# Expert routing by counted places in the first phase, and linear attention with its neighbours as one chain per batch

## Chip, cores, metric

One NeuronCore of a Trainium2 chip runs the whole program in one launch. The metric is the device time of that core in microseconds, the median of several runs; lower is better. The engines, with the names that the profile uses: TensorE (PE for matmuls, PEld for its weight loads), VectorE (DVE), ScalarE (ACT), GpSimd (POOL) and SyncE (SP, which issues most DMAs here; POOL issues the indirect ones). Each engine works off its own list of instructions in order and waits on semaphores for the others.

## What is computed

A stack of eight layers over x of 8 x 512 x 128 (4096 rows of 128 numbers, float32), each as x = x + layernorm(layer(layernorm(x))): softmax attention, a channel mix, a learning recurrence, a switch of experts, linear attention, a mixture of experts in which each expert picks its rows, attention with rotary positions, and a last set of experts. The change touches the three in the middle and the end of the third:

```python
# layer "L1_ffn": each row goes to its best expert, which keeps the first 256 rows that come
logits = x @ w_switch + b_switch
probs = jax.nn.softmax(logits, axis=-1); pmax = probs.max(axis=-1); routes = probs.argmax(axis=-1)
oh = (routes[:, None] == jnp.arange(E)[None, :]).astype(jnp.int32)
pos = (jnp.cumsum(oh, axis=0) * oh).sum(-1) - 1
keep = pos < capacity                                  # capacity = 4096 * 0.5 / 8 = 256
slot = jnp.where(keep, routes * capacity + pos, E * capacity)
buf = jnp.zeros((E * capacity + 1, D), x.dtype).at[slot].set(x)
h = jax.nn.relu(jnp.einsum('ecd,edh->ech', buf_e, w1) + b1[:, None, :])
y = jnp.einsum('ech,ehd->ecd', h, w2) + b2[:, None, :]
out = jnp.where(keep[:, None], y_flat[slot], x) * (pmax / stop_gradient(pmax))[:, None]

# layer "L2_attn": linear attention, 16 heads of 8
q, k = softplus(l2_normalize(q)), softplus(l2_normalize(k))
kv = einsum('bhnd,bhnc->bhdc', k, v) * scale;  ksum = k.sum(2) + EPS
out = einsum('bhnd,bhdc,bhn->bhnc', q, kv, 1 / einsum('bhnd,bhd->bhn', q, ksum))

# layer "L2_ffn": each of 8 experts takes the 512 rows that score highest for it
scores = softmax(xf @ gate_w.T);  vals, idx = top_k(scores.T, 512)
y = layernorm(xf[flat_idx]) * ln_w + ln_b
out = gelu(y @ fc1s.T + b1s) @ fc2s.T + b2s            # scaled by the score, added into xf
```

## The kernel before

Rows lie 128 to a tile; a batch b is 4 tiles (`NJ = 4`), held in SBUF as `cx.x[b]` (128 x 4 x 128) for the whole run. `flip` transposes 4 tiles on PE and copies them out of PSUM on ACT. A layernorm (`stats`, L164) is four bn_stats, four bn_aggr and an add on DVE and then a power on POOL (`ln_rs`, L176); it is applied by DVE (`norm`, L182) or by ACT (`norm_pieces`, L195).

Phase "first" (layers 0 to 3, L1459) has a hand-written order. `Attention.run` puts out the instructions of 128 groups of softmax attention, and between them `Background.pull` lets generators put out a piece each: `residuals`, `Mix.chain`, `Learn.chain` and `Learn.serve_chain`. A batch goes through them one after another; `Learn` is sequential over batches. `serve_chain` is one generator: for each batch in turn it adds the result of the learning layer to x (`served`) and then runs `Route.batch`, so batch b+1 is served behind all that `Route.batch(b)` puts out. `Route.batch` (L859 on) normalizes x, writes it to two tables in DRAM (`l1f_x` and `l1f_out`), and makes the eight logits of each row. When attention has no groups left, `bg.drain()` puts out the remaining pieces of the last batches; that stretch is called the tail here. `load` (L446) loads q, k, v for a group of attention by SP.

Phase "second" has no hand-written order in this version (`ring=0`): a scheduler may reorder within it.

- `l1_ffn` (L961 on): from all logits it finds each row's expert, lists for each expert the numbers of its first 256 rows (`listed`, L896: prefix sums on PE, comparisons on DVE), gathers these rows from `l1f_x` by indirect DMA on POOL (L953), runs the expert, and scatters its rows into `l1f_out` by indirect DMA on POOL (L1018). Then each batch is read back, scaled, normalized and added to x (L1028 to L1032).
- `l2_attn` (L1034 on): stage by stage over all 8 batches: projection for all, square root and reciprocal of all norms at once, exp for all, ln for all with the rest.
- `l2_ffn` (L1097 on): for each batch a layernorm, logits, softmax, a second layernorm scaled by `ln_w`, `ln_b`, and the rows into a DRAM table with their scores; then a search for each expert's 512th score bit by bit (30 rounds, L1152), the list of rows, and the experts with gathers (L953) and adding scatters (L1227).

Of the kernel before, what the change touches and what calls it, by code (L numbers as in the profile page):

```python
# [15 lines left out]
P = 128  # L16
B = 8
# [20 lines left out]
C_ALL = C_ROPE + NJ * 16  # L38
# [20 lines left out]
class Ctx:  # L59
# [104 lines left out]
    def stats(self, src):  # L164

        nc = self.nc
        st = self.common([P, NJ, 6], "ln_st", bufs=6)
        mv = self.common([P, NJ, 2], "ln_mv", bufs=6)
        for j in range(NJ):
            nc.vector.bn_stats(st[:, j, :], src[:, j, :])  # L170
        for j in range(NJ):
            nc.vector.bn_aggr(mv[:, j, :], st[:, j, :])
        ve = self.common([P, NJ], "ln_ve", bufs=6)
        nc.vector.tensor_scalar_add(ve, mv[:, :, 1], EPS)  # L174
        rs = self.common([P, NJ], "ln_rs", bufs=6)
        nc.gpsimd.tensor_tensor(rs, ve, self.mhalf[:, :NJ], ALU.pow)  # L176
        return mv, rs
# [8 lines left out]
    def norm_pieces(self, dst, src):  # L186

        nc = self.nc
        mv, rs = self.stats(src)
        yield 0.0, 1.5  # L190
        yield
        off = self.common([P, NJ], "ln_off", bufs=6)
        nc.vector.scalar_tensor_tensor(off, mv[:, :, 0], -1.0, rs, ALU.mult, ALU.mult)
        for j in range(NJ):
            nc.scalar.activation(  # L195
                dst[:, j, :], src[:, j, :], AF.Identity, bias=off[:, j : j + 1], scale=rs[:, j : j + 1]
            )
        yield
        yield
# [217 lines left out]
def l0(cx: Ctx, at: Attention, Wq, Wk, Wv, mix, learn):  # L417
# [28 lines left out]
    def load(n):  # L446
        b, j = divmod(n, NJ)
        if j == 0:
            bg.drain(projects[b])
            if b == 0:  # L450
                bg.add(mix.load())
                bg.add(learn.load())
            if b + 1 < B:
                projects[b + 1] = project(b + 1)
                bg.add(projects[b + 1])
# [387 lines left out]
class Route:  # L843


    def __init__(self, cx: Ctx, w_switch, b_switch):
        nc = cx.nc
        self.cx = cx
        self.w = cx.const([D, NE], "w1f_sw")
        nc.sync.dma_start(self.w, w_switch)  # L850
        self.bias = cx.row(b_switch, "w1f_bsw")
        self.table = cx.dram.tile([T, D], F32, name="l1f_x", tag="l1f_x")
        self.moved = cx.dram.tile([T, D], F32, name="l1f_out", tag="l1f_out")
        self.logits = cx.const([P, NT, NE], "l1f_logits")
# [4 lines left out]
    def batch(self, b):  # L859
        cx, nc = self.cx, self.cx.nc  # L860
        xn = cx.work([P, NJ, D], "l1f_xn", bufs=1)
        yield from cx.norm_pieces(xn, cx.x[b])
        nc.sync.dma_start(self.by_tile(self.table, b), xn)
        nc.sync.dma_start(self.by_tile(self.moved, b), xn)
# [4 lines left out]
        for j in range(NJ):  # L869
            nc.tensor.matmul(  # L870
                ps[:, j * NE : (j + 1) * NE], xt[:, j * P : (j + 1) * P], self.w, start=True, stop=True
            )
        nc.vector.tensor_add(
            self.logits[:, b * NJ : (b + 1) * NJ, :],
            ps[:, : NJ * NE].rearrange("p (j e) -> p j e", j=NJ),
            self.bias.unsqueeze(1).to_broadcast([P, NJ, NE]),
        )
        yield 0.8


def softmax_parts(cx: Ctx, name, logits):

    nc = cx.nc
    n = logits.shape[1]
    top = cx.work([P, n, 1], name + "_top")
    nc.vector.tensor_reduce(top, logits, AX.X, ALU.max)
    ex = cx.work([P, n, NE], name + "_ex")
    nc.vector.tensor_sub(ex, logits, top.to_broadcast([P, n, NE]))
    nc.scalar.activation(ex, ex, AF.Exp)
    inv = cx.work([P, n, 1], name + "_inv")  # L890
    nc.vector.tensor_reduce(inv, ex, AX.X, ALU.add)
    nc.vector.reciprocal(inv, inv)
    return top, ex, inv
# [67 lines left out]
def l1_ffn(cx: Ctx, route, w1, b1, w2, b2):  # L961
# [3 lines left out]
    cap = T // NE // 2  # L965
    ns = cap // P
    b1c = cx.columns(b1, "w1f_b1")
    b2b = cx.row(b2.rearrange("e d -> (e d)"), "w1f_b2")

    table, moved, logits = route.table, route.moved, route.logits  # L970
    by_tile = route.by_tile

    top, _, pmax = softmax_parts(cx, "l1f", logits)
    scale = cx.work([P, NT, 1], "l1f_scale", bufs=1)
    nc.vector.reciprocal(scale, pmax)
    nc.vector.tensor_mul(scale, scale, pmax)

    eq = cx.work([P, NT, NE], "l1f_eq")
    e8 = cx.c[:, C_E8 : C_E8 + NE].unsqueeze(1).to_broadcast([P, NT, NE])
    nc.vector.tensor_tensor(eq, logits, top.to_broadcast([P, NT, NE]), ALU.is_equal)  # L980
    nc.vector.tensor_mul(eq, eq, e8)
    best = cx.work([P, NT, 1], "l1f_best")
    nc.vector.tensor_reduce(best, eq, AX.X, ALU.min)
    sel = cx.work([P, NE, NT], "l1f_sel", bufs=1)
    nc.vector.tensor_tensor(sel.rearrange("p e t -> p t e"), e8, best.to_broadcast([P, NT, NE]), ALU.is_equal)
    idx = listed(cx, "l1f", sel, cap)
    put = as_indices(cx, "l1f_put", idx)
    nc.vector.tensor_scalar_min(idx, idx, float(T - 1))
    get = as_indices(cx, "l1f_get", idx)

    for e in range(NE):
        we1 = cx.work([D, F], "moe_w1", bufs=3)
        nc.sync.dma_start(we1, w1[e])
        we2 = cx.work([P, NF, D], "moe_w2", bufs=3)
        nc.sync.dma_start(we2, w2[e].rearrange("(f p) d -> p f d", p=P))
        t = cx.tr("l1f_xT_ps")
        for s in range(ns):
            xg = cx.work([P, D], "l1f_xg", bufs=4)
            gather(nc, xg, table, get[:, e, s : s + 1])
            nc.tensor.transpose(t[:, s * P : (s + 1) * P], xg, cx.ident)  # L1000
        xt = cx.work([D, cap], "l1f_xT")
        nc.vector.tensor_copy(xt, t[:, :cap])
        ht = cx.work([P, NF, cap], "l1f_hT")
        for f2 in range(NF // 2):
            hp = cx.big("l1f_h_ps")
            for i in range(2):
                f = 2 * f2 + i
                nc.tensor.matmul(hp[:, i, :cap], we1[:, f * P : (f + 1) * P], xt, start=True, stop=True)
                nc.scalar.activation(ht[:, f, :], hp[:, i, :cap], AF.Relu, bias=b1c[:, f, e : e + 1])
        yp = cx.acc("l1f_y_ps")  # L1010
        for s in range(ns):
            ss = slice(s * P, (s + 1) * P)
            for f in range(NF):
                nc.tensor.matmul(yp[:, ss], ht[:, f, ss], we2[:, f, :], start=(f == 0), stop=(f == NF - 1))
        for s in range(ns):
            y = cx.work([P, D], "l1f_y", bufs=4)
            nc.vector.tensor_add(y, yp[:, s * P : (s + 1) * P], b2b[:, e * D : (e + 1) * D])
            nc.gpsimd.indirect_dma_start(  # L1018
                out=moved,
                out_offset=bass.IndirectOffsetOnAxis(ap=put[:, e, s : s + 1], axis=0),  # L1020
                in_=y,
                in_offset=None,
                bounds_check=T - 1,
                oob_is_err=False,
            )
    for b in range(B):
        o = cx.work([P, NJ, D], "moe_o")
        nc.sync.dma_start(o, by_tile(moved, b))  # L1028
        for j in range(NJ):
            nc.vector.tensor_scalar_mul(o[:, j, :], o[:, j, :], scale[:, b * NJ + j, :])  # L1030
        cx.add_norm(b, o)


def l2_attn(cx: Ctx, W_qkv):  # L1034
    nc = cx.nc
    H = 16
    A = D + H
    w = cx.transposed(W_qkv, "w2a")
    bd = cx.c[:, C_BD : C_BD + A]
    heads = lambda t: t.rearrange("p j (h d) -> p (j h) d", d=8)  # L1040

    qks, vos = [], []
    norms = cx.work([P, B, P], "l2a_n", bufs=1)
    for b in range(B):
        _, xt = cx.normed_flipped(b)
        qk = cx.work([P, NJ, 2 * D], f"l2a_qk{b}", bufs=1)
        vo = cx.work([P, NJ, A], f"l2a_vo{b}", bufs=1)
        nc.gpsimd.memset(vo[:, :, D:], 1.0)
        for j in range(NJ):
            ps = cx.acc("l2a_qkv_ps")  # L1050
            nc.tensor.matmul(ps[:, : 3 * D], xt[:, j * P : (j + 1) * P], w, start=True, stop=True)
            nc.scalar.copy(qk[:, j, :], ps[:, : 2 * D])
            nc.vector.tensor_copy(vo[:, j, :D], ps[:, 2 * D : 3 * D])
        sq = cx.work([P, NJ, 2 * D], "l2a_sq")
        nc.gpsimd.tensor_mul(sq, qk, qk)
        nc.vector.tensor_reduce(norms[:, b, :].unsqueeze(2), heads(sq), AX.X, ALU.add)
        qks.append(qk)
        vos.append(vo)

    nc.vector.tensor_scalar_max(norms, norms, 1e-24)  # L1060
    nc.scalar.activation(norms, norms, AF.Sqrt)
    nc.vector.reciprocal(norms, norms)

    for b in range(B):
        nc.vector.tensor_mul(heads(qks[b]), heads(qks[b]), norms[:, b, :].unsqueeze(2).to_broadcast([P, P, 8]))
        nc.scalar.activation(qks[b], qks[b], AF.Exp)
    for b in range(B):
        sp, vo = qks[b], vos[b]
        nc.scalar.activation(sp, sp, AF.Ln, bias=1.0)
        kv = cx.acc("l2a_kv_ps")  # L1070
        for j in range(NJ):
            nc.tensor.matmul(kv[:, :A], sp[:, j, D:], vo[:, j, :], start=(j == 0), stop=(j == NJ - 1))
# [4 lines left out]
        cx.flip(qt, sp[:, :, :D])  # L1077
        op = cx.big("l2a_o_ps")
        for j in range(NJ):
            at = (j % 2) * A  # L1080
# [450 lines left out]
```

## Time and profile before

| what | us |
| --- | --- |
| median of 3 runs (lowest, highest) | 2361.89 (2356.22, 2367.21) |
| the profiled execution | 2359.79 |
| its span, first to last instruction | 2358.0 |
| start, to the first attention group | 0 to 31 |
| attention with layers 0 to 3 behind it | 31 to 735 |
| tail of the first phase | 735 to 886 |
| lists of rows for `l1_ffn` | 886 to 909 |
| its experts, to the last scatter | 909 to 973.5 |
| its rows added to x | 973.5 to 1018 |
| `l2_attn` | 1018 to 1137 |
| layernorms, logits and table of `l2_ffn` | 1137 to 1211.5 |
| search and list of `l2_ffn` | 1211.5 to 1322 |
| its experts and their sum into x | 1322 to 1505 |
| third phase (layers 6 and 7) | 1505 to 2358 |

The stages are read from the timeline by the first and last instruction that bears a stage's tile names. The clock that the page calls granted is TensorE's alone: 1.00 for most of both attention stretches, 0.5 where PE has little to do.

### The profile page before, as it was taken

To read this page: it belongs to the slowest core of one execution; us is meant where nothing else is said; L and a number is where in the kernel's file an instruction comes from. 1 tells how busy PE (TensorE), PEld (TensorE's weight loads), DVE (VectorE), ACT (ScalarE), POOL (GpSimd) and SP (SyncE) were. 2 spreads that over 40 slices of the span, in tenths; PEclk is the share of its full clock that TensorE was granted. 3 is DMA by queue.
4 is the path that set the end of the run, shared out by engine and by line. 5 is a ranking of instruction groups with operands and counts; after the bars stand their busy time and mean duration, and the time that the engine had idled before them with its cause. 6 is when DMAs were issued, how large, how long until landed. Compare 5 with 4: busy or idle time off the path is not lost. (4 is left out here: it accounts for less than half of the span.)

```text
span 2358.0 us, 31074 instructions
## 1 busy us (share of the span) xinstructions
PE 1880.9 (80%) x11232; PEld 955.4 (41%) x11232; DVE 1351.8 (57%) x4000; ACT 1094.5 (46%) x2178; POOL 479.3 (20%) x703
## 2 busy tenths in 40 slices
PE   6999999999998557144323773399999999999997
PEld 3334434444444446123222541133444444444455
DVE  3567676767765443386766311576565666755522
ACT  2667666565665312024000220056666666656653
POOL 2011121111111113342310264420111110200000
PEclk7999999999999656677555686599999999999999
DMA  3111111110100003100210232200000000000000
GB/s 91 36 32 21 27 31 22 31 36 17 22 19 17 9 30 106 39 9 0 68 33 0 50 50 28 72 1 1 1 1 5 1 5 1 6 1 6 5 6 9
DMA packets 143642, 55.71 MB, mean 24 GB/s; under 512 B 73307, under 2 KB 139527, under 8 KB 143489
## 3 DMA queue, kind: packets, MB, share of 16 engines
q1 hardware_dynamic: 136832, 47.43, 8.0%
q0 software_dynamic: 6656, 6.30, 1.7%
q8 instruction: 89, 1.46, 0.3%
q14 instruction: 65, 0.52, 0.1%
HBM read 31.68 MB, written 22.15 MB: 23 GB/s over the span
## 5 line engine op out<-in xcount | busy, mean ns | idle before, releaser
L336 DVE TENSOR_REDUCE pad_q<-at_s 128x1 f32<-128x512 f32 x1024 | 656.0, 684 | 392.9 <-PE at_st L342 326.0
L345 ACT ACTIVATE at_e<-at_st 128x512 f32<-128x512 f32 x1024 | 557.2, 594 | 402.3 <-PE at_st L342 387.6
L342 PE MATMUL at_st<-at_qm,at_k 32*128 32x512 f32 x2048 | 638.7, 646 | 6.6 <-DVE pad_q L336 5.8
L335 PE MATMUL at_s<-at_k,at_q 32*128 32x512 f32 x2048 | 590.2, 656 | 5.4 <-DVE pad_q L336 3.9
L176 POOL TENSOR_TENSOR ln_rs<-ln_ve,mhalf 128x4 f32<-128x4 f32 x136 | 138.0, 1014 | 821.7 <-DVE ln_ve L174 749.7
L354 PE MATMUL at_o<-at_e,pad_v 128*32 128x512 f32 x2048 | 280.1, 614 | 1.5 <-ACT at_e L345 1.4
L335 PEld LDWEIGHTS at_s<-at_k,at_q 32*128 32x128 f32 x2048 | 163.0, 188 | 250.8 <-issue 98.9
L342 PEld LDWEIGHTS at_st<-at_qm,at_k 32*128 32x128 f32 x2048 | 185.0, 184 | 60.6 <-DVE pad_q L336 40.8
L1423 PEld LDWEIGHTS l3f_y_ps<-w3f,l3f_hT 128*128 128x128 f32 x1024 | 126.4, 192 | 40.3 <-issue 23.7
L1423 PE MATMUL l3f_y_ps<-w3f,l3f_hT 128*128 128x128 f32 x1024 | 134.7, 278 | 0.8 <-ACT l3f_hT L1417 0.8
L1416 PE MATMUL l3f_h_ps<-l3f_xT,w3f 128*128 128x512 f32 x256 | 131.9, 607 | 1.5 <-ACT l3f_hT L1417 1.5
L354 PEld LDWEIGHTS at_o<-at_e,pad_v 128*32 128x32 f32 x2048 | 41.3, 108 | 199.0 <-issue 153.6
L1417 ACT ACTIVATE l3f_hT<-l3f_h_ps,w3f_b1c 128x512 f32<-128x512 f32 x128 | 87.8, 688 | 65.3 <-PE l3f_h_ps L1416 64.8
L1426 DVE SCALAR_TENSOR_TENSOR l3f_o<-l3f_y_ps,l3f_w,l3f_o 128x128 f32<-128x128 f32 x128 | 44.6, 349 | 118.4 <-PE l3f_y_ps L1423 117.5
L216 PE MATMUL flip<-consts_sb,xn 128*128 128x128 f32 x96 | 23.7, 366 | 100.2 <-DVE xn L182 91.1
L141 PE MATMUL wtr<-consts_sb,raw 128*128 128x128 f32 (+1 forms) x11 | 3.1, 412 | 99.4 <-DMA w3a_b<-in_L_attn_bqkv 67.9
L217 ACT COPY xnT<-flip 128x512 f32<-128x512 f32 x24 | 14.1, 587 | 130.7 <-PE flip L216 105.3
L1225 DVE TENSOR_TENSOR l2f_y<-l2f_y_ps,w2f_b 128x128 f32<-128x128 f32 x32 | 9.1, 290 | 94.0 <-DMA l2f_out<-l2f_y,l2f_get 78.3
L1147 PE MATMUL l2f_count_ps<-l2f_mine,ones 128*128 128x8 f32 x62 | 18.3, 368 | 56.1 <-DVE l2f_mine L1145 56.1
L1227 POOL DMA_INDIRECT l2f_out<-l2f_y,l2f_get x32 | 50.7, 1584 | 53.5 <-DMA l2f_out<-l2f_y,l2f_get 28.6
L216 PEld LDWEIGHTS flip<-consts_sb,xn 128*128 128x128 f32 x96 | 14.9, 166 | 114.2 <-DVE xn L182 58.4
L170 DVE BATCH_NORM_STATS2 ln_st<-x 128x6 f32<-128x128 f32 x256 | 58.1, 277 | 3.2 <-POOL x L838 3.2
(378 smaller groups left out, 2757.0 us busy)
## 6 DMA issues: line engine op xcount, KB each, us to landing
l_qkv<-l_qkv SPq DMA_DIRECT2D x32, 192.0 KB
l_in<-l_qkv SPq DMA_DIRECT2D x96, 64.0 KB
moe_w<-in_L_ffn_w SPq DMA_DIRECT2D x16, 256.0 KB
l2f_x<-l2f_rows SPq DMA_DIRECT2D x8, 272.0 KB
x<-in_L_attn_x SPq DMA_DIRECT2D x8, 256.0 KB
l_o<-l_out SPq DMA_DIRECT2D x32, 64.0 KB
l_y<-l_o SPq DMA_DIRECT2D x32, 64.0 KB
l1f_x<-l1f_xn SPq DMA_DIRECT2D x8, 256.0 KB
```

The source lines that it names most:

```text
L170: nc.vector.bn_stats(st[:, j, :], src[:, j, :])
L176: nc.gpsimd.tensor_tensor(rs, ve, self.mhalf[:, :NJ], ALU.pow)
L335: nc.tensor.matmul(s, qt[n][r, c * P : (c + 1) * P], kt[n][r, :], start=True, stop=True)
L336: nc.vector.tensor_reduce(qp[:, c, h, 8:9], s, AX.X, ALU.max, negate=True)
L342: nc.tensor.matmul(s, kt[n][r, c * P : (c + 1) * P], qm[n][r, :], start=True, stop=True)
L345: nc.scalar.activation(es[g][:, h, :], s, AF.Exp, scale=scale)
L354: nc.tensor.matmul(os[n][32 * h : 32 * h + 32, :], vp[:, c, h, :], e[:, h, :], start=(c == 0), stop=(c == NJ - 1),)
L1227: nc.gpsimd.indirect_dma_start(out=summed, out_offset=bass.IndirectOffsetOnAxis(ap=idx[:, e, s : s + 1], axis=0), in_=y, in_offset=None, c ...
L1416: nc.tensor.matmul(hp, self.w1[:, e, f * P : (f + 1) * P], xt, start=True, stop=True)
L1417: nc.scalar.activation(hts[e][:, f], hp, AF.Relu, bias=self.b1c[:, f, e : e + 1])
L1423: nc.tensor.matmul(yp[:, :D], hts[e][:, f, js], self.w2[:, e, f, :], start=(f == 0), stop=(f == NF - 1))
L1426: nc.vector.scalar_tensor_tensor(o[:, j, :], yp[:, :D], wt[:, j, e : e + 1], o[:, j, :], ALU.mult, ALU.add)
```

## The change

In the first phase `Route.batch` goes on after the logits: softmax parts, the best expert of each row, its place among the expert's rows by matmuls with a triangle and with ones (11 per batch, with a count carried from batch to batch), and four indirect DMAs on POOL that scatter the batch's rows into a DRAM block per expert (`taken`); a row without a place gets a number out of bounds, which is skipped. `clear` writes zeros to `taken` by 8 DMAs of 128 KB on SP, ahead of the first loads for attention. The second copy of the table is gone.

`l1_experts` replaces `l1_ffn`: it loads each expert's 256 rows as a plain block, runs the experts in a hand-written order two steps apart, and stores a plain block (`given`). The lists, the gathers and the scatters of `l1_ffn` are gone. Loads of rows are put out ahead of the loads of weights on SP.

`Pairs.batch` takes together the sum of `l1_ffn` into x, `l2_attn`, and the first part of `l2_ffn`, as one generator of 29 steps per batch. `in_turn` starts a batch every 7 rounds and lets each running batch put out one step per round, the oldest first; this order is kept. Layernorms are applied by ACT throughout; the norms are found by ln and exp instead of square root and reciprocal, with one set of activation functions loaded ahead; squares move from POOL to ACT; `ln_w` and `ln_b` move into the experts' weights in `l2_ffn`.

```diff
 class Route:
...
+    def clear(self):
+        for e in range(NE):
+            self.cx.nc.sync.dma_start(self.taken[e * CAP1 : (e + 1) * CAP1, :]..., self.zero...)
     def batch(self, b):
...
-        nc.sync.dma_start(self.by_tile(self.moved, b), xn)
...
+        top = tile_of("top", 1)
+        nc.vector.tensor_reduce(top, logits, AX.X, ALU.max)
+        ex = tile_of("ex")
+        nc.vector.tensor_sub(ex, logits, top.to_broadcast(by_expert))
+        nc.scalar.activation(ex, ex, AF.Exp)
+        yield 0.8, 0.6
+        eq = tile_of("eq")
+        nc.vector.tensor_tensor(eq, logits, top.to_broadcast(by_expert), ALU.is_equal)
+        nc.vector.tensor_mul(eq, eq, e8)
+        nc.vector.tensor_reduce(best, eq, AX.X, ALU.min)
+        nc.vector.tensor_tensor(sel, e8, best.to_broadcast(by_expert), ALU.is_equal)
+        yield 0.0, 0.6
+        nc.tensor.matmul(ps[:, : NJ * NE], cx.triu, sel.rearrange("p j e -> p (j e)"), start=True, stop=False)
+        for j in range(NJ):
+            for i in range(j + 1, NJ + 1):
+                nc.tensor.matmul(ps[:, i * NE : (i + 1) * NE], cx.ones, sel[:, j, :], start=False, stop=(j == NJ - 1))
...
+        nc.vector.tensor_scalar_add(self.place[:, tiles].unsqueeze(2), best, float(FAR))
+        yield 1.3, 0.9
...
+        for j in range(NJ):
+            nc.gpsimd.indirect_dma_start(out=self.taken, ... in_=xn[:, j, :], ...)
+            yield 0.0, 0.2
...
     def load(n):
         if j == 0:
             bg.drain(projects[b])
             if b == 0:
+                learn.route.clear()
                 bg.add(mix.load())
...
+def l1_experts(cx: Ctx, route, w1, b1, w2, b2):
+    for e in range(NE):
+        xg = cx.work([P, ns, D], "l1f_xg", bufs=NE)
+        nc.sync.dma_start(xg, of_expert(route.taken, e))
...
+    for e in range(4):
+        weights(e)
+    for e in range(NE + 2):
+        if e < NE:
+            taken(e)
+        if 0 <= e - 1 < NE:
+            hidden(e - 1)
+        if 0 <= e - 2 < NE:
+            given(e - 2)
+            if e + 2 < NE:
+                weights(e + 2)
+def in_turn(gens, gap):
+    waiting, running = list(gens), []
+    n = 0
+    while waiting or running:
+        if waiting and n % gap == 0:
+            running.append(waiting.pop(0))
+        for g in list(running):
+            try:
+                next(g)
+            except StopIteration:
+                running.remove(g)
+        n += 1
+class Pairs:
+    def batch(self, b):
+        o = tile_of("o")                                            # steps 1, 2
+        nc.sync.dma_start(o, route.by_tile(route.table, b))
+        for j in range(NJ):                                         # steps 3, 4 (and 5, empty)
+            nc.gpsimd.indirect_dma_start(out=o[:, j, :], in_=route.given, ...)
+        mv = cx.moments(o)                                          # 6: and three small DVE ops
+        rs = cx.root(ve)
+        cx.affine(t, o, rs, cx.offset(mv, rs))                      # 7
+        nc.gpsimd.tensor_add(x, x, t)                               # 8
+        mv, rs = cx.stats(x)                                        # 9
+        cx.affine(xn, x, rs, cx.offset(mv, rs))                     # 10
+        cx.flip(xt, xn)                                             # 11
+        nc.tensor.matmul(ps[:, : 3 * D], xt[:, block(j)], self.w)   # 12, 13: two blocks each
+        nc.scalar.copy(qkv[:, j, : 3 * D], ps[:, : 3 * D])
+        nc.scalar.activation(sq, qk, AF.Square)                     # 14: and four sums, a max on DVE
+        nc.scalar.activation(nf, nf, AF.Ln)                         # 15
+        nc.scalar.activation(nf, nf, AF.Exp, scale=-0.5)
+        nc.vector.tensor_mul(v, v, n[:, j, :]...)                   # 16: four
+        nc.scalar.activation(qk, qk, AF.Exp)                        # 17
+        nc.scalar.activation(qk, qk, AF.Ln, bias=1.0)               # 18
...
+        cx.flip(qt, qkv[:, :, :D])                                  # 19: behind kv and m; 20 is empty
+        nc.tensor.matmul(op[:, k * A : (k + 1) * A], qt[:, block(j)], m)   # 21: and rec, product on DVE
+        mv, rs = cx.stats(o)                                        # 22
+        cx.affine(t, o, rs, cx.offset(mv, rs))                      # 23
+        nc.gpsimd.tensor_add(x, x, t)                               # 24
+        mv, rs = cx.stats(x)                                        # 25
+        rs2 = cx.root(ve)                                           # 26: behind three small DVE ops
+        cx.affine(xn, x, rs, cx.offset(mv, rs))
+        cx.flip(xt, xn)                                             # 27: and the store of xn
+        cx.affine(rows, x, rs2, cx.offset(mv, rs2), D)
+        nc.tensor.matmul(ps[:, j * NE : (j + 1) * NE], xt[:, block(j)], self.gw)   # 28: top, sub, exp
+        nc.sync.dma_start(route.by_tile(self.table, b), rows)       # 29: behind the scores
...
 def l2_ffn(...):
...
         cx.flip(we1, raw1)
+        bp = cx.acc("l2f_b_ps")
+        for f in range(NF):
+            nc.tensor.matmul(bp[:, f : f + 1], we1[:, f * P : (f + 1) * P], lb, start=True, stop=True)
+        nc.vector.tensor_add(be1, bp[:, :NF], b1c[:, :, e])
+        nc.gpsimd.tensor_scalar_mul(we1, we1, lw)
...
     with cx.phase("second"):
+        with cx.layer("layer3", ring=8):
+            l1_experts(cx, route, *of("L1_ffn", "w1", "b1", "w2", "b2"))
+        with cx.layer("layer4", ring=8):
+            tc.keep_in_program_order(nc.scalar.preload_act_table_set("natural_log_exp_and_others"))
+            pairs = Pairs(cx, route, *of("L2_attn", "W_qkv"), *of("L2_ffn", "gate_w"))
+            in_turn([pairs.batch(b) for b in range(B)], 7)
```

The steps of `Pairs.batch` are numbered here for the text; a step is what lies between two `yield`s.

## The prediction

> **What bounds the kernel now.** I read the page's slices first, then busy time by stage, then the timeline where the change works. The slices say whether one engine bounds the whole run:
>
> ```profile
> PE   6999999999998557144323773399999999999997
> DVE  3567676767765443386766311576565666755522
> ACT  2667666565665312024000220056666666656653
> PEclk7999999999999656677555686599999999999999
> ```
>
> PE is full in slices 2 to 12 and in the last 14: those stretches are bound by it. Between them (about 735 to 1505 us) no engine is full and TensorE's granted clock falls to a half: latency and waits set the time. The change works there and adds to the first stretch. By stage (columns: stretch, its length, then busy us and instructions of PE, PEld, DVE, ACT, POOL, then clock, DMA share, GB/s):
>
> ```profile
> 31.00:735.00 704.00, 688.33 (x4360) 300.16 (x4360) 486.92 (x1230) 444.30 (x907) 105.48 (x200) 0.96 0.13 27
> 735.00:886.00 151.00, 89.14 (x429) 68.72 (x427) 61.38 (x245) 43.25 (x99) 25.06 (x25) 0.62 0.08 23
> 886.00:909.20 23.20, 13.77 (x45) 10.14 (x45) 15.78 (x62) 2.96 (x17) 0.76 (x9) 0.50 0.26 77
> 909.20:973.50 64.30, 38.28 (x211) 31.24 (x211) 8.05 (x25) 14.12 (x32) 31.57 (x32) 0.79 0.25 72
> 973.50:1211.50 238.00, 83.48 (x357) 62.19 (x357) 173.40 (x752) 48.40 (x85) 81.47 (x72) 0.63 0.11 33
> ```
>
> The fourth row is bound by none of its engines. The timeline of POOL shows by what:
>
> ```profile
> 965.24 0.98 POOL L1018 DMA_INDIRECT l1f_out<-l1f_y,l1f_put  x1 [2.00 <-issue]
> 968.23 0.98 POOL L1018 DMA_INDIRECT l1f_out<-l1f_y,l1f_put  x1 [2.01 <-DMA l1f_out<-l1f_y,l1f_put]
> 971.14 0.98 POOL L1018 DMA_INDIRECT l1f_out<-l1f_y,l1f_put  x1 [1.93 <-DMA l1f_out<-l1f_y,l1f_put]
> ```
>
> Each scatter waits until the one before it has landed: 3.0 us from start to start though POOL works 0.98. Their data was ready (the last y was written at 961.6). 16 of them make 48 of the stage's 64 us.
>
> **The sum** is made against the profiled execution, 2359.8 us (span 2358.0 and 1.8 around it); the median of the runs, 2361.9, is 2.1 above.
>
> **1. Zeros at the start.** `clear` puts 8 DMAs on SP between the stores of q, k, v (last issue 25.2) and the first loads for attention:
>
> ```profile
> 25.68 4.92 SPq L460 DMA_DIRECT2D l_in<-l_qkv  x9
> 28.12 0.29 POOL L319 COPY pad_q<-l_in 128x128 f32<-128x128 f32 x1 [11.94 <-DMA l_in<-l_qkv]
> ```
>
> A store of 256 KB by SP took 0.36 to 0.51 us to issue (L863, L864), so the loads are issued 8 x 0.43 = 3.4 us later, with 1 MB of zeros before them: in the first 12.5 us about 2.6 MB (constants, x) landed within 10 us, so 1 MB takes about 4 us, mostly under the issues. POOL's copies wait for the loads and the first scores for them; after that PE is full, so nothing makes it up. +5 (3 to 8).
>
> **2. Place-finding inside attention.** `l1f_xn` is stored at 401, 506, 604, 699 and, in the tail, 759, 813, 863, 883: four batches fall under attention. Each adds 11 small matmuls. Nearest are the logits' four (8 records):
>
> ```profile
> 703.47 1.06 PE L870 MATMUL l1f_log_ps<-w1f_sw,l1f_xnT 128*128 128x8 f32 x8
> 884.23 1.88 PE L870 MATMUL l1f_log_ps<-w1f_sw,l1f_xnT 128*128 128x8 f32 x8 [0.68 <-ACT l1f_xnT L217]
> ```
>
> 0.265 us each at full clock, 0.47 at half. 4 x 11 x 0.265 = 11.7 on an engine busy 688 of 704. Some fills gaps: +10 (0 to 12). The 17 DVE operations of some 0.2 us (3.4 per batch) hide under PE while DVE is busy 487 of 704; with PE not full they would cost those 14 us. POOL's scatters stand between `fill` copies put out eight groups ahead and hide too.
>
> **3. Place-finding in the tail.** Here nothing hides: three more batches (4, 5, 6) put 11 x 0.47 = 5.2 us of matmuls into PE's queue, and DVE's next addition waits for them with the learning chain's operations queued behind it. For batches 4 and 5 I take +4 and +5. Batch 6 is worse: batch 7 is served behind it, and its layernorm's power stands in POOL's queue behind batch 6's four scatters:
>
> ```profile
> 874.27 1.01 POOL L176 TENSOR_TENSOR ln_rs<-ln_ve,mhalf 128x4 f32<-128x4 f32 x1 [13.71 <-DVE ln_ve L174]
> ```
>
> Logits of batch 6 at 866.2, choice of experts six small operations to 867.5, matmuls behind each other to 874, places 876, scatters at 876.3, 879.3, 882.3, 885.3: the power comes at 886.4 for 874.3, +12. Sum +20; 8 if the three matmul groups fit PE's idle time, 28 if every wait counts in full.
>
> **4. From the last logits to the experts' last row.** Before: 886.15 to 973.5, 87.3 us. After: choice 1.4, matmuls 5.2, places 1.3, then four scatters at 3.0 and 1.4 to be seen (971.14 + 0.98 to SP's 973.49): 19.7 to the first load of rows. SP then issues 8 loads, b1, b2, and only behind them weights (before, these came at 886.9, ahead of need): 1.8 MB at 260 GB/s from 906 brings the first weights at 915, 9 us on. The experts run at PE's pace of before's unhindered ones, 4.15 us (929.99, 934.14, 938.29 start hidden layers), the first 2.2 more at half clock: 36; addition, store, landing 3. Together 68: -19 (-27 to -12; weights and clock decide). [...]
>
> **5. The chain.** By rows, one batch costs ACT 16.0 us (five affines at 1.65, three copies 0.58, four 0.48, three of 1024 at 1.04, small ones 0.9) where it had 48.4/8 = 6.0; DVE 14.7; POOL 13 (gathers 1.25, powers 1.01, additions 1.27). With four batches in turn the period per batch T is at least 16. The order is kept, so I laid seven rounds out by hand, from the oldest batch's step 23: affine to 1.85; POOL's addition 24 stands behind the power of a younger batch's step 9, which follows the products 16 and its own bn_stats on DVE (3.3): 5.7; stats 25 to 7.2; its power stands behind two gathers (2.5): 9.2; small operations and affine 26: 11.7; ACT's copies 19 and 12: 13.3; copy 27: 13.9; ACT's affine of the rows, two copies, exp, square of step 14: 17.8; four sums of 256 at 0.41 and a max: 19.8; steps 7, 29 and 22 on DVE: 22.3; power: 23.4. At half clock PE's 4 x 1.28 for the projection, 2.2 for kv and so on add 4.5: 27.9. PE would be busy 37%, where 1070 to 1137 (39%) had clock 0.68; T = 25.
>
> The first batch reaches step 23 at 51 (alone but for two young ones), five full periods make 125, the next two, with fewer beside them, 23.5 and 18.5, the last seven steps 14: 232 (219 to 255) for 238 now. -6 (-19 to +17).
>
> **6. Experts of `l2_ffn`.** Each gets one POOL product of 128x512 (between a memset's 0.52 and an addition's 1.27) among scatters 3.6 to 4.1 apart, where gathers already fill most waits; its four matmuls and DVE addition hide under that chain. +3 (0 to +10).
>
> Sum: 5 + 10 + 20 - 19 - 6 + 3 = +13; 2373, beside the median 2374. ±0.5% (12 us) is what a measurement here can tell from no change. The main case's own range is 2358 to 2412.
>
> **Rivals.** *The chain runs at ACT's pace* (T about 17; for it: ACT and DVE alone would allow it, and 29 steps times four batches leave choice; against: the order is fixed and POOL's gathers stand in it): 51 + 7 x 17 + 14 = 184 for 232, 2326. It ends on the faster side as soon as T is under 25 - 25/6.7 = 21.3. *The additions to the first phase vanish* (PE's matmuls fill gaps, the tail takes +6): 10 + 14 less, 2350; for it: PE idles 62 of 151 us in the tail; against: the in-order waits above. *Functions are switched* (exp and ln alternate; the one set does not hold): four loads per batch at the 1.28 of L1066 and L1069, 41 us, of which ACT's slack hides some 5: 2410; against: a set was asked for by name. [...] At L1066 the trace shows the next activation 0.02 us behind the load.
>
> **Chances.** Main case 0.45, T at ACT's pace 0.20, first phase unharmed 0.27, switched functions 0.08. Slower by over 0.5%: 0.36 of the main case, 0.08 of the last, 0.01: 0.45. Faster: 0.18 and 0.11: 0.29. The rest, 0.26, is within. The range takes in most of the faster rival and the bounds above that can meet: 2322 to 2414.
>
> **What will show it.** First scores at 36 instead of 31. Attention's end at 750 and the last logits near 921. Four scatters 3.0 apart behind them, the first transposes of rows about 20 us later. In the chain, powers of step 25 behind gathers on POOL, ACT at two thirds, steps 23 of neighbouring batches 25 us apart (under 21 and I am wrong on the sign), one function load. The search about 13 us later than 1211.5, and the rest unchanged from there but for the experts of `l2_ffn`.

## The result, and the profile after

Twenty runs of each kernel on one chip gave a median of 2374.52 us (2365.75 to 2383.55) for the changed kernel and 2362.14 us (2352.2 to 2367.87) for the one before. The ratio is 1.0056, with a 95% interval of 1.0041 to 1.0072: the change costs some 12 us. The forecast was 2374. The profiled execution of the changed kernel has a span of 2370.5 us (2358.0 before), 12.5 more.

The total hides larger moves. From the first and last starts of a few groups in the two profiles (us):

| stretch | before | after | difference | forecast |
|---|---|---|---|---|
| start to the first scores | 31.1 | 36.2 | +5.1 | +5 |
| attention, to its last output | 718.0 | 736.6 | +18.6 | +10 |
| tail, to the last logits | 137.0 | 152.6 | +15.6 | +20 |
| logits to the first experts' last row | 87.4 | 65.6 | -21.8 | -19 |
| add and linear attention, to the first count of the search | 239.0 | 224.6 | -14.4 | -6 |
| search | 72.1 | 72.1 | 0 | 0 |
| lists, to the first gather | 37.1 | 39.6 | +2.5 | +3 for both |
| experts of `l2_ffn` | 146.7 | 151.6 | +4.9 | |
| sum, start of the third phase | 104.2 | 108.2 | +4.0 | 0 |
| third phase, from its first outputs | 785.4 | 783.4 | -2.0 | 0 |

The page of the changed kernel, its slices (40 equal ones; PE's busy tenths, and the granted clock of TensorE in tenths):

```profile
PE   5999999999999563544333773299999999999998
PEclk7999999999997665766655686589999999999999
```

Attention still fills PE. But the last slice of attention that is full (711 to 770 us) has a clock of 0.7 where it was 0.9. The same kernel by stage (stretch, its length, then busy us of PE, PEld, DVE, ACT, POOL, then clock, DMA share, GB/s):

```profile
36.20:772.80 736.60, 720.35 (x4501) 316.57 (x4502) 498.84 (x1295) 451.72 (x922) 121.14 (x217) 0.94 0.12 25
772.80:925.40 152.60, 88.82 (x443) 75.13 (x441) 67.78 (x292) 37.56 (x90) 37.24 (x36) 0.61 0.03 9
925.40:991.00 65.60, 39.19 (x238) 35.92 (x238) 17.71 (x52) 9.10 (x18) 4.39 (x9) 0.73 0.45 128
991.00:1211.50 220.50, 89.29 (x352) 65.08 (x352) 114.41 (x551) 120.01 (x264) 93.52 (x88) 0.62 0.10 29
```

In the chain (last row) ACT, the busiest engine, works 54% of the time: as before, no engine is full there.

**Attention.** Weighting each 5 us of attention with its granted clock gives the time lost to a clock under 1.0: 26.8 us before, 44.0 after, 17.2 more. PE's work at full clock, what is left of its busy time, is 674.0 and 676.4, its idle time 17.2 and 16.3. By this measure +18.6 is 17.2 of clock and 2.4 of work, less 0.9 of idle time. The kernel before, over the same stretch (to be held against the first row above):

```profile
31.10:749.10 718.00, 700.80 (x4438) 306.14 (x4438) 492.11 (x1248) 452.63 (x923) 107.71 (x203) 0.96 0.12 26
```

The split is a rough one: of PE's 4501 records 88 are new, in four groups that alone hold PE for 11.3 us, while 25 others no longer fall within it. The timeline shows the largest loss, at the fourth group:

```profile
733.14 0.65 PE L332 MATMUL at_qm_ps<-consts_sb,pad_q 128*128 128x128 f32 x4
733.63 0.31 PE L939 MATMUL l1f_rank_ps<-l1f_sel,consts_sb 128*128 128x32 f32 x2
733.78 3.07 PE L944 MATMUL l1f_rank_ps<-l1f_sel,ones 128*128 128x8 f32 x20
736.78 2.08 PE L364 MATMUL at_st<-at_qm,at_k 32*128 32x512 f32 x4
```

and busy time and clock in the stretches of that group and behind it:

```profile
733.60:736.80 3.20, 3.20 (x26) 3.18 (x24) 0.00 (x0) 1.21 (x3) 0.00 (x0) 0.76 0.02 5
736.80:745.00 8.20, 8.20 (x28) 3.53 (x28) 1.10 (x7) 3.33 (x8) 2.03 (x2) 0.50 0.02 7
745.00:757.50 12.50, 12.50 (x42) 4.26 (x46) 5.98 (x22) 4.83 (x10) 2.26 (x2) 0.50 0.06 13
```

Place-finding puts 22 records on PE (11 matmuls, two records each in this trace), 20 of them 8 columns wide. Over the group the clock is 0.76, and behind it 0.50 for 21 us of attention's own matmuls, though PE is busy without a gap: the four `at_st` take 2.08 us instead of 1.13.

**Tail.** Batch 7 behind batch 6's scatters (DVE and POOL):

```profile
903.64 1.04 POOL L968 DMA_INDIRECT l1f_taken<-l1f_xn,l1f_place  x1 [14.82 <-DVE l1f_place L960]
908.10 0.17 DVE L174 TENSOR_SCALAR ln_ve<-ln_mv 128x4 f32<-128x4 f32 x1
912.45 0.97 POOL L968 DMA_INDIRECT l1f_taken<-l1f_xn,l1f_place  x1 [1.96 <-DMA l1f_taken<-l1f_xn,l1f_place]
913.43 1.06 POOL L180 TENSOR_TENSOR ln_rs<-ln_ve,mhalf 128x4 f32<-128x4 f32 x1
```

The variance is there at 908.27; the power that reads it starts at 913.43, in POOL's queue behind the fourth scatter: 5.2 us.

**First experts.** From the last logits (925.4):

```profile
945.02 3.94 SPq L1053 DMA_DIRECT2D l1f_xg<-l1f_taken  x8
949.01 0.41 SPq L161 DMA_DIRECT2D raw_b<-in_L_ffn_b  x1
949.87 0.42 SPq L1065 DMA_DIRECT2D l1f_w<-in_L_ffn_w  x1
951.82 0.57 PE L165 MATMUL col<-consts_sb,raw_b 8*128 8x8 f32 x4 [20.07 <-DMA raw_b<-in_L_ffn_b]
952.32 1.11 PE L1071 MATMUL l1f_xT_ps<-consts_sb,l1f_xg 128*128 128x128 f32 x4
955.70 3.75 PE L1082 MATMUL l1f_h_ps<-l1f_xT,l1f_w 128*128 128x256 f32 x8 [2.27 <-DMA l1f_w<-in_L_ffn_w]
```

The first load of rows is issued 19.6 us behind the logits, the first weights are there at 955.7; then one expert takes 3.73 us (from 963.84 to 967.57).

**Chain.** One period, from one addition L1196 to the next (POOL and DVE alone, in extracts):

```profile
1086.94 1.26 POOL L1196 TENSOR_TENSOR x<-x,l_t 128x512 f32<-128x512 f32 x1
1088.15 1.42 DVE L1233 TENSOR_TENSOR l2a_qkv<-l2a_qkv,l2a_n 128x256 f32<-128x256 f32 x4
1090.91 1.02 POOL L180 TENSOR_TENSOR ln_rs<-ln_ve,mhalf 128x4 f32<-128x4 f32 x1 [2.71 <-DVE ln_ve L174]
1091.90 1.26 POOL L1273 TENSOR_TENSOR x<-x,l_t 128x512 f32<-128x512 f32 x1
1091.96 1.22 DVE L197 SCALAR_TENSOR_TENSOR ln_off<-ln_mv,ln_rs 128x4 f32<-128x4 f32 x1 [1.13 <-POOL ln_rs L180]
1094.70 1.00 POOL L1172 DMA_INDIRECT l_o<-l1f_given,l1f_place  x1 [0.30 <-issue]
1095.72 1.05 POOL L180 TENSOR_TENSOR ln_rs<-ln_ve,mhalf 128x4 f32<-128x4 f32 x1
1102.61 1.00 POOL L180 TENSOR_TENSOR ln_rs<-ln_ve,mhalf 128x4 f32<-128x4 f32 x1 [2.21 <-DVE ln_ve L1189]
1103.67 0.19 DVE L1299 TENSOR_REDUCE l2f_top<-l2f_log_ps 128x4 f32<-128x32 f32 x1 [1.20 <-PE l2f_log_ps L1296]
1110.75 1.26 POOL L1196 TENSOR_TENSOR x<-x,l_t 128x512 f32<-128x512 f32 x1
```

The work passes between DVE and POOL for most of the period; PE and ACT take part too, as at 1103.67, where DVE waits 1.20 us for PE. The power at 1095.72 stands behind two gathers; the small `ln_off` at 1091.96, elsewhere 0.16 us, lasts until POOL's addition ends. The period is 23.8 us.

### The profile page after: what moved, and what is told of

The parts are those of the page before. It is cut to its first block, busy times and chain, and to the rows that moved or that the text cites. A ratio compares the mean times of both kernels' runs of the same rounds, so it can differ in the third digit from the quotient of the medians.

```text
span 2370.5 us, 31595 instructions
## 1 busy us (share of the span) xinstructions
PE 1913.9 (81%) x11432; PEld 987.0 (42%) x11432; DVE 1307.8 (55%) x3890; ACT 1160.3 (49%) x2333; POOL 505.3 (21%) x724
## 5 line engine op out<-in xcount | busy, mean ns | idle before, releaser
L364 PE MATMUL at_st<-at_qm,at_k 32*128 32x512 f32 x2048 | 649.2, 656 | 10.1 <-DVE pad_q L358 9.9
L238 PE MATMUL flip<-consts_sb,l_xn 128*128 128x128 f32 x96 | 26.6, 367 | 121.4 <-ACT l_xn L203 120.3
L238 PEld LDWEIGHTS flip<-consts_sb,l_xn 128*128 128x128 f32 x96 | 14.0, 158 | 139.2 <-ACT l_xn L203 131.9
L203 ACT ACTIVATE l_xn<-x,ln_off,ln_rs 128x128 f32<-128x128 f32 x96 | 39.5, 483 | 48.1 <-DVE ln_off L197 43.8
L334 ACT COPY at_q<-at_q_ps 128x512 f32<-128x512 f32 x64 | 37.7, 589 | 40.8 <-PE at_q_ps L332 40.8
```

The lines of the kernel that those rows point to most:

```text
L238: self.nc.tensor.transpose(t[:, j * P : (j + 1) * P], src[:, j, :], self.ident)
L364: nc.tensor.matmul(s, kt[n][r, c * P : (c + 1) * P], qm[n][r, :], start=True, stop=True)
```

## The experiments

**Places with fewer, wider matmuls.** The ten matmuls of 8 columns per batch become one of 32 for the totals, added up on DVE:

```
-        for j in range(NJ):
-            for i in range(j + 1, NJ + 1):
-                nc.tensor.matmul(ps[:, i * NE : (i + 1) * NE], cx.ones, sel[:, j, :], ...)
+        nc.tensor.matmul(ps[:, NJ * NE : 2 * NJ * NE], cx.ones, sel.rearrange("p j e -> p (j e)"), ...)
+        for j in range(NJ):
+            nc.vector.tensor_add(rank[:, j + 1, :], rank[:, j, :], tot[:, j, :])
```

> The ten matmuls of 8 columns per batch become one of 32 columns, and five small operations of DVE add the totals up (20 fewer instruction records of PE per batch, 1 us more on DVE). Theory A (the short matmuls cost their own time, 2.4 us per batch, and TensorE's clock, which the trace of the changed kernel shows at a half behind all four groups that lie in attention): attention's last output from 772.8 to about 755; each batch of the tail some 3 us earlier; places of the last batch at 4 us behind its logits instead of 7; 2374 falls to 2335 to 2350. Rival B (they cost their own time alone, and the halved clock comes from elsewhere): attention's last output at 764, halved clock behind the places as before; 2350 to 2362. Rival C (attention's length is set by the extra work on DVE and POOL, not by PE): no earlier than 770, and no gain over 8 us.

2356.68 us, ratio to the kernel before 0.9959 (0.9939 to 0.998). Attention's last output at 763.5, the last logits at 906.0 (925.4 in the changed kernel), the last places 4.4 us behind them (7.4). The clock lost in attention is 29.4 us. The size is B's (763.5 for its 764); the mechanism has to be told from the next run, since work and clock both went.

**As many matmuls, but wide.** The same, and nine matmuls per batch of 128 columns whose result nobody reads:

```
+        for i in range(9):
+            nc.tensor.matmul(ps[:, 2 * P : 3 * P], cx.ones, cx.ident, start=True, stop=True)
```

> As the run before, but with nine more matmuls of 128 columns per batch behind the two, whose result nobody reads: as many instructions of PE as in the changed kernel and about the same time of PE (0.117 us a record against 0.107), but 16 times the columns. Theory A (few columns per matmul are what lets the clock fall): the clock stays at full behind the groups in attention, attention's last output at 762 to 767, between the run before and the changed kernel. Rival B (a group of 22 records of any kind, or the stop of attention's own matmuls for 2.4 us, does it): the halved clock stays, last output at 771 to 776.

2374.37 us, ratio 1.0032 (1.0013 to 1.0051). Attention's last output at 764.8, clock lost 31.9. The same group there, and the stretch behind it:

```profile
732.26 2.25 PE L947 MATMUL l1f_rank_ps<-consts_sb,ones 128*128 128x128 f32 x18
734.44 1.13 PE L364 MATMUL at_st<-at_qm,at_k 32*128 32x512 f32 x4
```

```profile
734.50:745.00 10.50, 10.50 (x65) 4.18 (x64) 6.90 (x24) 7.43 (x17) 4.30 (x4) 1.00 0.03 9
```

PE is held for 2.6 us by 22 records as in the changed kernel, and the clock stays at 1.0. Over the profiles: in the changed kernel and the seven others here that keep its groups of 8 columns, a clock of 0.75 or less follows in the 3 us behind 27 of 32 groups in attention; behind the four wide ones it is 1.0 for 12 us, and behind the four short ones of the run before 0.91 or more (two of these fall later: one 3 us on, where the kernel before had a fall too, at 635 to 645, and the last one 6 us on). So in these runs the fall follows groups of 8 columns (27 of 32) and not groups of 128 (none of 4) that hold PE as long: theory A.

It is not the whole of what attention lost. Up to the 30th of its 32 outputs (at 712 us in the kernel before) the three forms lie close together: 12.8 us behind the kernel before with the narrow matmuls, 11.9 with the short, 9.6 with the wide ones, some 5 of it from the start. The last two outputs, with the fourth group among them, add 10.9, 2.5 and 6.1. So that one group in its narrow form costs 5 us more than in the wide and 8 more than in the short one; another 5 to 8 us came with every form, and no run here shows from what. (In the tail, where the changed kernel's clock is 0.50 in each group and in the 3.5 us ahead of it, this profile has 161.7 us, between the 152.5 and 164.4 of the narrow form, and the median can't be told from the changed kernel's.)

**Zeros later.** `clear` is called in front of the second batch's loads.

```
+            if b == 1:
+                learn.route.clear()
```

> The eight stores of zeros move from in front of the first loads for attention to in front of the second batch's. My step 1 (they delay the first loads): first scores at 31 instead of 36.2, and the end 5 us earlier, 2369. Rival (the gain is taken back: in the new place they delay loads that attention waits for, or the first groups' clock swallows it): first scores at 31, but attention's last output at 771 or later.

First scores at 31.4, but attention's last output at 774.0 and the clock lost 47.1 us; 2373.28 us, ratio 1.0043 (1.0021 to 1.0065), which can be told neither from the changed kernel's 1.0056 nor from 5 us (0.2%) less. By its own mark the rival holds, in one profile: the 5 us are real where they arise, and in this execution they were lost by attention's end. By which of its two reasons, and whether the median keeps them, stays open.

**Weights in front of rows.** In `l1_experts` the biases and the first four experts' weights are asked for ahead of the rows.

> In the first experts' stage the first four experts' weights and the biases are asked for ahead of the eight loads of rows on SP's queue instead of behind them. Theory (the first hidden layer at 955.7 waits for weights, my step 4): first hidden layer some 6 us sooner after the last scatter (942.5 to 955.7 is 13.2 us in the changed kernel, 7 here), end at 2368. Rival 1 (the weights' buffers come free only with the last scatter, so that the loads of rows now stand behind weights): 13 us or more, end at 2374 to 2378. Rival 2 (1 MB more in flight beside the row loads delays these by as much as it gains): 11 to 13.

2371.82 us, ratio 1.0034 (1.0013 to 1.0056). Last scatter to first hidden layer 15.5 us instead of 13.2. SP's queue of that run:

```profile
954.20 0.35 SPq L161 DMA_DIRECT2D raw_b<-in_L_ffn_b  x1
955.01 0.42 SPq L1060 DMA_DIRECT2D l1f_w<-in_L_ffn_w  x1
960.14 5.72 SPq L1108 DMA_DIRECT2D l1f_xg<-l1f_taken  x8
```

The last scatter was issued at 951.6. Nothing of the stage is asked for before it has landed, and the rows now come last. The times are rival 1's. But the wait stands at the first load in the queue, the biases', issued 2.6 us behind the last scatter (954.2 for 951.6) as the first load of rows is in the changed kernel (945.02 for 942.46); whether the weights' buffers would have held their loads too, this run doesn't show. (The tail was 164.4 us in this profile, with the very instructions that took 152.6 in the changed kernel's; two more profiles with that code had 152.5, one 164.4. Differences of that size in one profile's tail are no reading.)

**Early weights.** The first four experts' weights get tiles that stay, and are asked for behind the store of batch 6's rows.

> Only the early weights: tiles that stay for the first four experts' weights, asked for behind the store of batch 6's rows, some 60 us ahead of need. Theory (the run with weights ahead of rows lost because the buffers came free only with the first phase's end, not because of the order): places to first hidden layer 16 to 18 us instead of 22.9 in the changed kernel, median 2368. Rival (the loads of rows, the biases' columns and the half clock make the wait, weights or not): 21 or more, median 2374.

2370.74 us, ratio 1.0038 (1.0019 to 1.0057); places to first hidden layer 20.8 us: nearly the rival's. The weights' wait is gone, but PE's first instruction there is the transposes of the biases, whose load stands behind the eight loads of rows (at 949.51; they run at 952.72). The last run moves that load.

**The chain's additions on DVE.**

```
-        nc.gpsimd.tensor_add(x, x, t)
+        nc.vector.tensor_add(x, x, t)
```

> In the chain the two additions of a block to x go from POOL (1.26 us each) to DVE. Theory L (the chain's period, 23.8 us from one batch's addition 24 to the next, is one path that changes between DVE and POOL, in the order the program was written): both additions lie on that path, and DVE's small operation beside each is drawn out from 0.16 to 1.22 us; on DVE an addition of this size takes some 0.7, so the period falls by 1 to 3 us, to 21 to 23, and the chain (first gather to last scores, 220.6 us) to 200 to 213. Rival A (ACT's affines set the period): 23.8 stays. Rival D (DVE is the scarcer engine: 1.4 us more on it per batch): 24 to 25.5, chain 222 to 232.

2353.28 us, ratio 0.996 (0.9938 to 0.9981). The chain takes 210.1 us from first gather to last scores, the period is 22.3 (mean of five). In it:

```profile
1098.85 0.69 DVE L1273 TENSOR_TENSOR x<-x,l_t 128x512 f32<-128x512 f32 x1
1100.43 0.16 DVE L197 SCALAR_TENSOR_TENSOR ln_off<-ln_mv,ln_rs 128x4 f32<-128x4 f32 x1 [0.90 <-POOL ln_rs L180]
```

The addition takes 0.69 and `ln_off` is 0.16 again, in all 40 cases. ACT's work did not change (120.5 us busy for 120.0), so ACT's pace did not set the period. DVE was busy 110.6 us for 114.5: the shorter small operations more than pay for the additions. That is theory L, at its low end. The median gained more than the chain's 10.5 us: by the two ratios to the kernel before some 23 us lie between this run and the changed kernel, and the profile, of the slowest of its ten executions, doesn't show where the rest arose.

**The chain's powers on ACT.**

```
-        self.nc.gpsimd.tensor_tensor(rs, ve, self.mhalf[:, :NJ], ALU.pow)
+        self.nc.scalar.activation(rs, ve, AF.Ln)
+        self.nc.scalar.activation(rs, rs, AF.Exp, scale=-0.5)
```

> In the chain the six powers per batch go from POOL (1.02 us each) to ACT as two activations of 0.3 (a logarithm and an exponential, in the set already loaded). Theory L (DVE and POOL in turn set the period): the path loses up to 0.4 us and the waits behind POOL's gathers and additions at each power, but ACT's affines stand ahead now: 20 to 24. Rival A (ACT sets the period): ACT gets 3.6 us more per batch, period 26 to 28, chain 235 to 250.

2363.39 us, ratio 1.0 (0.9982 to 1.0019). Chain 217.1 us, period 23.4 (mean of five). ACT was busy 132 us instead of 120 and the period did not grow: against rival A again. It hardly fell either; whether what is won behind POOL's gathers is lost behind ACT's affines wasn't separated. Here too `ln_off` takes 0.16 us in 39 of 40 cases (in the changed kernel 12 of 40 take 1.2), so the drawn-out operation alone is not what set the period. By the ratios this run is some 13 us faster than the changed kernel, of which the chain accounts for 3.5; the rest isn't explained.

**Scale on DVE.** In the experts of `l2_ffn` the product `we1 * lw` moves to DVE.

> In the last experts' stage the product of the first weights with the norm's scale (POOL, 1.6 us, eight times) goes to DVE. My step 6 (it stands among POOL's gathers and scatter-adds): first gather 1.6 to 2.8 us sooner after the search's end (39.1 us in the changed kernel, 36.6 before), and the stretch from the first gather to the loads of the sums 147 to 149 instead of 151.6 (146.7 before). Rival (the stretch is longer because of the four added matmuls and the clock): 151 or more.

One run, 2362.65 us. First gather to the loads of the sums 148.0 us: POOL's share is borne out, by a little (nine profiles without this edit have 149.5 to 152.1, the two later runs that have it 146.8 and 147.8). But the first gather came 39.4 us behind the search's last count (39.6 in the changed kernel), no sooner:

```profile
1319.72 0.16 DVE L1397 TENSOR_TENSOR l2f_b<-l2f_b_ps,w2f_b 128x4 f32<-128x4 f32 x1 [1.33 <-PE l2f_b_ps L1395]
1319.91 0.48 DVE L1398 TENSOR_SCALAR l2f_w<-l2f_w,w2f_lnw 128x512 f32<-128x512 f32 x1
1320.31 0.18 DVE L1031 CAST l2f_get<-l2f_idx 128x32 int32<-128x32 f32 x1
```

The first expert's bias addition, which waits for PE, stands in DVE's queue ahead of the conversion that the gathers need; the product has only joined it there.

**Scatters that needn't wait.** Each of a batch's four tiles goes to a table of its own; the experts read the first alone.

> The four tiles of each batch are scattered to four tables instead of one; the experts read only the first of them, so three quarters of the rows that they should get are zeros (the work is the same). Theory W (each scatter waits for the one before it, since all write one table: 2.9 us apart, of which POOL works 0.98): 1.2 to 1.5 us apart, the last batch's four in 4 to 5 us instead of 8.7, and its power no longer 5.2 us late behind the batch before: last scatter 8 to 10 us earlier. Rival Q (POOL's queue or the writing of the descriptors takes 2.9 whatever the target): 2.5 us or more apart, nothing gained.

One run, 2363.74 us. The last batch's scatters:

```profile
932.10 1.03 POOL L971 DMA_INDIRECT l1f_taken<-l1f_xn,l1f_place  x1 [13.41 <-DVE l1f_scale L969]
933.44 0.98 POOL L971 DMA_INDIRECT l1f_part<-l1f_xn,l1f_place  x1 [0.30 <-issue]
934.73 0.97 POOL L971 DMA_INDIRECT l1f_part<-l1f_xn,l1f_place  x1 [0.30 <-issue]
936.00 0.97 POOL L971 DMA_INDIRECT l1f_part<-l1f_xn,l1f_place  x1 [0.30 <-issue]
```

1.3 us apart instead of 2.9: the wait is for the one table (theory W). Places to first hidden layer 18.8 us instead of 22.9. Batch 7's power now follows its variance by 0.09 us instead of 5.2, and from batch 6's logits to batch 7's it is 26.0 us instead of 30.9. The last scatter came 6.5 us earlier, not 8 to 10; the tail as a whole was 155.1 us. This form does not give the right rows, and one that does was not tried.

**The kernel before again.**

> The kernel before once more, to see how far a single profile of it goes. Theory (its first phase is shorter than the changed kernel's because the clock is lost less): attention's last output at 747 to 755, lost clock in attention near 27 us, and no half clock for over 12 us on end after 600. Rival (the first profile was a lucky one): 758 or more.

Attention's last output at 750.4, clock lost 27.4, the tail 137.1: the first profile was no lucky one. From the loads of the last experts' sums to the third phase's first outputs it takes 108.2 us, where the first profile had 104.2. Five profiles with the changed kernel's first phase have 731.6 to 738.1 us in attention (37.8 to 44.9 of them lost to the clock) and 152.5 to 164.4 in the tail.

**Together.** Wider place-finding, additions and scale on DVE, early weights.

> Four edits together: places by one matmul of 32 columns for the totals; the chain's additions on DVE; the last experts' product with the scale on DVE; the first four experts' weights of the first experts' stage in tiles of their own, asked for while the last batches are routed. If each does what it did alone, and the early weights bring what the wait for them was (some 6 us): last attention's output near 763, chain near 210 us, the last experts' stretch 148, places to first hidden layer 16 to 18 us instead of 22.9; median 2374 - 18 - 10 - 3 - 6 = 2337 (2328 to 2345). Rival (in the chain and the experts the clock takes part back, as it did in attention): 2345 to 2355.

2342.46 us, ratio 0.9922 (0.9901 to 0.9943). Attention's last output at 762.5, clock lost 27.2; places to first hidden layer 20.4; chain 210.2; experts of `l2_ffn` 146.8. The median lies in the theory's range (2328 to 2345). The parts hold together; the early weights brought 2.5 instead of 6.

**And two more.** The biases' load in front of the rows', and the chain's powers on ACT.

> The four edits together and two more: the first experts' biases, whose transposes stand ahead of the experts' on PE, are loaded ahead of the eight loads of rows; and the chain's powers on ACT, now with the additions on DVE, so that POOL has only gathers there. Theory (the biases' load, issued 4 us behind the first rows', is what the early weights left waiting): places to first hidden layer 16.5 to 18.5 us instead of 20.4. Rival (the rows themselves come no sooner): 20 or more. Chain: if POOL's powers behind gathers still cost on the path, 195 to 205 us instead of 210; if ACT takes the place of POOL, 208 to 215. Median 2342 - 3 - (0 to 10): 2329 to 2341.

2331.5 us, ratio 0.9865 (0.984 to 0.9889): 1.35% faster than the kernel before, and the best here. Places to first hidden layer 15.9 us, so the biases were the wait. Chain 206.1 us, period 22.0: between the two cases. DVE, ACT and POOL are busy 110, 132 and 32 of these 206 us; what sets the period now stays open.

## Why the prediction was right

The time was 2374.5 for 2374, and the sign and most mechanisms hold, but part of the agreement is errors that cancel: +8.6 in attention, +4.4 at the last experts and +2 behind them, against -4.4 in the tail, -2.8 at the first experts and -8.4 in the chain. That these cancel to within 1 us is luck: at the first count of the search the changed kernel was 3.1 us behind, where the first five terms add up to 10.

- **1, zeros.** +5.1 at the first scores, as worked out. Whether the total pays it, the run with `clear` moved leaves open.
- **2, place-finding inside attention** is the step that was mis-sized: "4 x 11 x 0.265 = 11.7", taken as +10 with 12 as its upper end. Measured +18.6, outside the bounds. I priced the matmuls by their duration and looked for the gaps they fill; left out was the clock behind them. 10.9 us of the growth come with the last two outputs, behind the fourth group, where the short matmuls add 2.5 and the wide ones 6.1. With as many records and more columns attention took 728.9, against 731.6 to 738.1 in five profiles with the narrow ones and 718.0 before; the 5 to 8 us that every form has stay unexplained. That DVE's new operations are hidden holds: the run with short matmuls puts more of them on DVE (504 us busy for 499) and its attention is 9 us shorter.
- **3, tail.** +15.6 for +20. The order of waits is as drawn: places behind PE's small matmuls (4.9 us at a clock of 0.50), four scatters, the power of batch 7 behind them, 5.2 us late. From batch 6's logits to batch 7's it is 30.9 us for 20.0, +10.9 where 12 was expected; batches 4 to 6 together make 4.6 of the expected 9. Two other profiles with the same instructions have 164.4 in the tail, which would be +27.4; all of that difference lies ahead of batch 6's logits, so the forecast for batch 7 is the firm part. With short matmuls the tail was 142.5.
- **4, to the experts' last row.** -21.8 for -19. First load of rows 19.6 behind the logits (19.7 forecast, though its terms as written add up to 19.3 or to 21.3, by how the fourth scatter is counted); the first transposes of rows came 27 us behind them, not about 20; the experts then took 3.73 us each where 4.15 was taken from the disturbed stage before. That scatters wait for one another through their table is shown by the four tables (1.3 us apart instead of 2.9). "Weights 9 us on" was near as a time (10.7) and not the cause alone: the biases' transposes stood almost as late, and with their load moved forward the wait fell by 4.5 us.
- **5, chain.** The period came to 23.8 for 25 (bounds 23.4 to 27.9), the first batch's addition 24 at 53.6 where step 23 was put at 51, the end 10.6 after the last addition 24 where 14 was put behind step 23; ACT was busy 54% for two thirds; in all -14.4 for -6. The mechanism, an order in which gathers, powers and additions on POOL stand in DVE's way, is borne out in part by the additions moved to DVE; the powers moved to ACT brought little. The rival at ACT's pace is out: 21.3, where it would have changed the sign, was not reached, and two runs speak against ACT as the bound.
- **6, experts.** +7.4 over lists and experts for +3, inside 0 to 10. Missed was the bias addition in DVE's queue, and the product took 1.59 us on POOL, above the 0.52 and 1.27 it was put between.
- **Behind the experts,** +4.0 to the third phase's first outputs and -2.0 from there. The +4.0 is not the change's: the kernel before again takes the same 108.2 us there. The -2.0 was not foreseen and isn't explained.
- **Other rivals.** Switched functions: the trace has four function loads of 1.28 us in the whole kernel, seven before; one is at 984.7, ahead of the chain, and none in it. That the first phase's additions vanish: it grew by 39 us.

## What to carry to other kernels

The matmuls put among TensorE's full work had two prices here: their time (3.2 us for the fourth group) and the clock of the work behind them (0.50 for 21 us). Gather narrow products into few wide ones, even at the cost of small sums on another engine: here that alone turned 0.56% slower into 0.41% faster. Where engines take turns in a fixed order, try the steps that make one wait for the other on another engine, one kind at a time: in the chain the additions brought 10.5 us, the powers 3.5. And before moving a load forward, see what has to come free for it: here the loads moved ahead of the rows were still issued 2.6 us behind the last scatter (954.2 for 951.6).

## What was unexpected of the hardware

- TensorE's clock fell with PE busy at every moment. 22 records of mostly 8 columns in 2.5 to 3.2 us were followed by a clock of 0.75 or less in the 3 us behind 27 of 32 groups in attention (1.00 behind the other five), and behind the fourth group of the changed kernel it stayed at 0.50 for 21 us under matmuls that filled PE, most of that time 32*128 or 128*32 in the trace. 22 records of 32 and 128 columns in 2.6 to 2.8 us were followed by 1.00 for 12 us, four times of four. What sets the clock, no run here shows.
- The same instructions in the tail took 152.6 us in the changed kernel's profile and 164.4 in that of the run with weights in front of rows, with mean clocks of 0.61 and 0.55; PE was busy 88.8 and 100.5 us with 443 records in both.
- A small DVE operation that starts beside POOL's addition of 128x512 lasted until that ended: 1.22 us for 0.16, in 12 of 40 cases in the chain, all 12 ending within 0.03 us behind the addition; in none of 40 with the additions on DVE.
